# A two-layer graph network in fp32 on one core: new places for the weights, the first three and the last two graphs

## The chip, the core and the metric

The kernel runs on one core of a Trainium2 chip. The metric is the device time of one execution in microseconds (us). The program uses five instruction streams: TensorE (PE in the profile; its weight loads are listed apart as PEld), VectorE (DVE), ScalarE (ACT), GpSimd (POOL), and SyncE (SP), which here only issues DMAs. Each stream runs its instructions strictly in the order in which they were written; an instruction that has to wait holds up all that stand behind it in its stream.

## The reference, cut to what matters

There are 64 graphs of 256 nodes with 512 features each, in fp32. All graphs use the same weights: W0 (512 x 1024), Wv (512 x 512), aw (1024 x 1), Wk (3 x 512 x 512), and three small biases.

```python
# layer 0
h = relu(layernorm(x))                                  # over the 512 features
agg = (adj @ h) / max(sum(adj, -1), 1e-6)
x = x + relu(concat([h, agg], 2) @ W0.T)

# layer 1
h = relu(layernorm(x))
Xw = h @ Wv + bv
e = leaky_relu((Xw @ aw[:512])[:, None, :] + (Xw @ aw[512:])[:, :, None] + ab, 0.2)
alpha = adj * exp(e)
T = alpha / (sum(alpha, -1) + 1e-12)                    # "transition"
H = h @ Wk[0] + bk[0] + (T @ h) @ Wk[1] + bk[1] + (T @ (T @ h)) @ Wk[2] + bk[2]
out = x + relu(H)
```

## The kernel before, in words

**The arithmetic.** All the large products are taken apart in Strassen's manner: a product of two matrices in 2x2 blocks becomes seven block products, with sums of blocks of the left and the right factor before, and sums of the results behind. Weights are combined once at the start and stay in SBUF (`W0F`, `W1F`, `WQF`; the profile calls them all `l` or `lq`). For each graph TensorE makes products of 256 columns with a weight tile of 128x128, each in one step from SBUF to a PSUM bank; VectorE and ScalarE pass the partial sums between banks and SBUF, and GpSimd makes most of the sums of the left factors and some sums of results. The layer-1 product is regrouped: h times v (v is Wv times the two halves of aw, in two rows) gives the two scores of a node without forming Xw, and T·(h·Wk[1] + T·h·Wk[2]) is summed in one set of banks with h·Wk[0].

**The stages of a graph**, with the names that are used below (lines of the kernel before):
- `prepare` (L534): `norm_relu` (L316) on x: row sums with ScalarE, the scaling of the mean `sm` (POOL, L329), squares (ACT, L331), the variance and its power -0.5 (POOL, L333 and L334), then the scaled ReLU (ACT, L337), giving h in tile `h0`. `scaled` (near L520) divides the adjacency by its row sums. Both must then be transposed. For graphs 0 and 1, `flip_on_pe` (L363) does this with TensorE transposes into a bank and copies out of it; for the others, `put` (L340) transposes blocks of 32x32 on VectorE (L345) and writes them to DRAM by DMAs on SP (L349), and `get` (L353) reads them back in the transposed order in the stage `prepared` (L545).
- `wide` (L555): h times both halves of W0, as a scheme of 26 products. `LEFT_SUMS` are 18 sums of 128x128 blocks of h-transposed, one instruction each (L387 on VectorE or L389 on GpSimd); `EARLY` (graphs 0 and 1, banks 3 to 6) and `STEPS` (the others, banks 0 to 2) list the products and the passing of the partial sums: P a product, S a copy to a staging tile, D, T and O sums, F a copy back to a bank.
- `layer0` (L597): the aggregation as seven products through `main` (L494) on banks 0 to 2, started by its "fifth" product; `finish` (L512) adds the ReLU of the banks to x (L516).
- `turn1` (L607): layernorm and ReLU of the new x, four dot products with the v rows on VectorE (L613), and `put` of h to DRAM.
- `transition` (L622): the column of scores goes out and comes back as a row through DRAM (L624, L625); four exponentials (L630), the maximum of the two branches (L633), two products with the adjacency, the scaling, and the transposition: for graphs 1 to 61 through DRAM, for graph 0 and the last two on TensorE (`tt.flip`, L373).
- `moved`, `once`, `inner`, `turned1`, `outer` (from L647): the sums of the transition (tile `st`), `spread` (L446, T times h as seven pairs of 128x128 products on banks 6 and 7, giving `zg`), `inner` (L659, banks 6 and 7, times the third weight, giving `qf`), the read of h-transposed, and `outer` (L687, banks 3 to 5, everything added up), whose `finish` and one DMA of 512 KB per graph (L694) store the output.

In a turn of the loop, `moved` to `outer` run for the graph before, `prepare` and `prepared` for the next graph, and the loads of x and adjacency (L314) for the graph three ahead.

**The order of the work.** Nothing is ordered by the compiler. Each operation is recorded by `Plan.add` (L200) with its engine and the tiles that it reads and writes. `emit` (L222) sorts the operations of each engine by a place, and writes them in that order:

```python
at = self.base + (times[self.count] if self.count < len(times) else 0.0)   # base: graph * TURN + SHIFT
for i in sorted(range(len(self.ops)), key=lambda i: self.ops[i][3]):       # emit
```

The places stand in the table `AT`, a row for each stage; graphs 0 to 2 have rows of their own (`wide_0`), graphs 62 and 63 in two stages, and `SHIFT` moves whole stages of the last four graphs. A place decides only the order in a stream, not a time. The costs given to `add` have no effect on the program.

**The start.** `first` (L823) loads x of graph 0 in halves. `weights_l0` (L708) loads W0 in four parts of 512 KB (L712), transposes it with 8 groups of four transposes into banks 1, 2 and 0 in rotation (L725), and copies each half bank to SBUF by ScalarE (16 copies, L731 and L733). `combine0` (L736) makes 28 sums of these pieces on VectorE. `weights_l1` (L744) loads and transposes Wv (L775), copies it (L777), and multiplies it with aw: aw is broadcast to a 128-wide tile (L768), so that each of the two products of 512 columns gives a v row already repeated in all 128 partitions. Then `combine` (L698, L703) forms sums of Wk, and bk is spread by one product with ones. `pool_op` (L385) decides which of the sums run on VectorE instead of GpSimd: all those of graph 0, and `zg`, `qf` and `st` of graph 1.

Of the kernel before, what the change touches and what calls it, by code (L numbers as in the profile page):

```python
# [11 lines left out]
AF = mybir.ActivationFunctionType  # L12
# [13 lines left out]
TURN = 44.55  # L26
AT = {
    "first": (-1017.24, -941.27, -1067.90, -979.42, -1133.31, -1447.98, -1153.03, -1322.56, -861.36, -1000.46, -1271.51, -1112.17, -1031.96,
        -1007.46, -997.64, -1019.48, -995.91, -966.87, -807.55, -710.53, -781.12, -671.89, -691.05, -715.55, -741.64, -649.04, -668.80, -637.21,
        -513.09, -573.30, -611.16, -532.37, -616.22, -652.18, -1057.15, -794.26, -597.00, -1140.64, -889.40, -650.49, -823.54, -717.73, -1031.47,  # L30
        -761.68, -747.99, -593.69, -583.75, -527.52, -656.78, -632.97, -239.87, -431.83, -275.83, -1179.40, -946.09, -433.84, -905.70, -638.56,
        -569.10, -880.53, -782.04, -705.59, -492.83, -421.05, -288.74),
    "inner": (112.00, 118.30, 113.21, 111.00, 119.38, 119.48, 120.51, 123.95, 119.91, 117.78, 125.62, 122.20, 129.97, 123.35, 122.08, 122.94, 143.35),
    "inner_0": (120.04, 124.14, 111.34, 108.02, 121.17, 121.28, 127.27, 128.59, 125.03, 116.12, 137.98, 117.98, 127.36, 129.02, 121.84, 124.49,
        158.46),
    "inner_1": (116.30, 120.49, 114.79, 118.55, 119.44, 121.25, 125.68, 131.77, 125.03, 121.31, 129.70, 128.89, 139.17, 129.13, 123.63, 129.21,
        153.96),
    "inner_2": (117.14, 119.66, 118.60, 112.70, 119.26, 121.13, 124.83, 125.54, 119.49, 118.09, 129.51, 123.19, 123.50, 122.53, 120.98, 119.85,
        132.84),
    "layer0": (8.82, 12.23, 23.66, 30.27, 32.06, 29.03, 34.55, 32.01, 36.75, 34.14, 40.29, 34.61, 40.44, 41.44, 41.62, 36.17, 36.49),  # L40
    "layer0_0": (-200.51, -154.12, -17.22, -72.28, 8.54, -32.05, 23.63, -26.42, 30.82, -16.30, 32.72, -9.73, 34.62, 34.67, 35.87, -8.32, -3.57),
    "layer0_1": (-17.97, 4.41, -34.79, 12.11, 32.36, 15.72, 43.05, 22.64, 44.10, 24.61, 47.37, 27.04, 47.39, 47.89, 48.17, 27.25, 27.35),
    "layer0_2": (16.51, 27.98, 24.87, 29.85, 39.27, 28.73, 40.14, 29.55, 40.49, 31.62, 41.67, 35.42, 41.84, 41.86, 44.64, 35.47, 36.33),
    "loads": (-73.25, -54.78),
    "loads_2": (-570.55, -440.31),
    "moved": (96.10, 94.60, 90.90, 91.65, 92.10, 98.61),
    "moved_0": (74.40, 78.92, 73.46, 86.50),
    "moved_1": (91.74, 94.49, 96.28, 96.47, 101.59, 99.65),
    "moved_2": (92.45, 93.46, 87.17, 93.36, 88.66, 95.64),
    "moved_late": (277.68, 282.26, 301.99, 292.62),  # L50
    "once": (54.49, 60.96, 71.27, 72.69, 100.45, 102.13, 97.01, 101.40, 103.69, 104.26, 107.89, 108.15, 102.72, 101.65, 111.96, 103.21, 108.87,
        104.14, 109.67, 110.05, 110.23),
    "once_0": (61.39, 68.65, 43.72, 76.81, 102.31, 108.28, 88.12, 81.94, 109.93, 110.01, 111.86, 113.88, 100.99, 87.31, 97.51, 91.16, 118.80, 101.72,
        103.42, 103.65, 107.11),
    "once_1": (66.98, 69.71, 84.14, 73.11, 100.43, 102.58, 97.12, 100.84, 104.63, 106.78, 110.21, 112.55, 110.97, 102.83, 112.58, 108.30, 112.06,
        106.52, 108.00, 110.24, 114.90),
    "once_2": (48.31, 85.20, 76.99, 85.55, 99.90, 100.10, 96.57, 97.65, 102.25, 103.85, 102.31, 107.68, 98.75, 105.26, 111.34, 111.29, 114.34,
        108.24, 109.43, 112.02, 115.28),
    "outer": (110.55, 112.56, 124.59, 130.71, 122.70, 126.64, 130.05, 124.51, 132.31, 132.69, 134.42, 130.55, 136.29, 137.75, 137.79, 134.66, 140.16,
        142.97, 144.27, 143.30, 141.14, 144.88, 147.05, 147.31, 154.75, 166.76, 149.89, 152.90, 180.04, 173.32, 178.81, 183.03),  # L60
    "outer_0": (75.64, 100.62, 136.69, 136.53, 104.98, 130.05, 133.80, 126.65, 135.71, 136.92, 137.86, 135.82, 139.47, 140.60, 141.14, 138.11,
        143.83, 144.28, 144.84, 145.15, 143.50, 148.77, 148.79, 152.22, 164.19, 164.74, 149.82, 155.17, 176.64, 177.49, 176.45, 180.92),
    "outer_1": (116.86, 117.84, 128.53, 124.70, 122.55, 133.39, 134.11, 129.95, 135.65, 136.44, 136.94, 134.18, 139.81, 139.88, 141.12, 136.84,
        143.12, 148.89, 149.66, 146.81, 143.91, 148.56, 149.77, 153.75, 159.49, 159.72, 152.49, 156.26, 164.38, 167.52, 171.63, 187.33),
    "outer_2": (109.82, 117.34, 125.19, 132.21, 122.42, 127.44, 130.36, 123.94, 131.81, 132.14, 134.85, 131.51, 136.29, 138.25, 138.62, 135.11,
        140.08, 141.11, 142.64, 144.31, 139.88, 144.08, 146.43, 149.56, 150.02, 152.80, 151.35, 151.79, 159.27, 158.56, 152.70, 181.89),
    "prepare": (-58.85, -58.04, -62.77, -50.47, -50.61, -50.10, -47.67, -44.00, -35.79, -33.31, -40.71, -40.92, -34.53, -30.46, -9.67, -12.00,
        -30.84, -30.59, -19.83, -17.85, -13.42, -16.63, -13.01, -0.86, -2.11, 0.02, -0.84),
    "prepare_0": (-1266.53, -975.17, -811.01, -687.47, -880.33, -683.51, -631.06, -581.34, -621.45, -471.77, -1128.62, -1029.34, -1034.44, -882.61,
        -476.14, -489.14, -495.72, -471.07, -383.05, -399.08),  # L70
    "prepare_1": (-557.96, -458.29, -573.61, -253.06, -248.24, -448.75, -390.09, -379.42, -209.99, -190.33, -642.97, -325.85, -355.58, -242.70,
        -180.44, -173.98, -131.68, -163.72, -123.16, -162.03),
    "prepare_2": (-239.11, -208.13, -283.36, -178.85, -105.45, -128.88, -95.37, -80.24, -60.94, -70.06, -131.95, -63.34, -57.66, -46.88, -50.72,
        -47.06, -39.69, -38.58, -74.39, -50.57, -47.70, -74.26, -35.20, -31.13, -44.27, -36.41, -25.44),
    "prepared": (-10.65, 2.40, -0.87),
    "prepared_0": (-266.03, -448.40, -238.28, -282.28),
    "prepared_1": (-42.49, -39.69, 9.83, -23.75),
    "prepared_2": (-15.15, -0.37, 11.90),
    "transition": (55.63, 60.89, 66.16, 59.33, 66.37, 62.85, 61.19, 61.54, 61.61, 62.29, 62.78, 69.44, 69.86, 65.50, 84.98, 85.82, 78.93, 86.06),
    "transition_0": (-37.87, -34.45, 59.61, 61.95, 59.61, 59.97, 69.12, 70.02, 69.57, 70.91, 71.09, 73.37, 74.08, 94.36, 73.26, 95.01, 76.83),  # L80
    "transition_1": (41.14, 59.01, 60.68, 59.69, 61.21, 66.18, 58.69, 58.69, 58.88, 60.76, 61.81, 69.31, 69.66, 62.81, 83.27, 81.85, 79.74, 81.08),
    "transition_2": (48.98, 68.97, 59.08, 59.45, 64.06, 66.35, 59.35, 61.89, 61.81, 62.34, 62.37, 69.62, 73.39, 66.89, 81.35, 84.81, 82.67, 86.91),
    "transition_late": (-54.45, -49.51, 1.31, -11.56, 5.58, 1.28, 1.86, 18.81, 4.03, 18.88, 19.04, 24.08, 44.52, 30.73, 24.06, 60.74, 64.88),
    "turn1": (34.41, 40.31, 39.20, 37.21, 37.30, 39.30, 43.54, 44.94, 46.57, 47.03, 54.64, 55.20, 55.64, 56.82, 51.30, 51.88, 64.71, 63.98, 58.81,
        56.74),
    "turn1_0": (-37.13, -10.01, -7.88, -26.00, -25.40, -17.44, 11.38, 11.78, 24.35, 28.13, 30.44, 32.22, 43.73, 49.19, 23.26, 23.32, -152.13, -56.73,
        -93.40, -120.59),
    "turn1_1": (23.38, 31.87, 33.04, 29.38, 31.30, 34.45, 39.81, 41.29, 33.66, 34.98, 42.54, 47.50, 58.19, 58.12, 39.23, 35.62, 58.55, 66.38, 62.43,
        46.18),
    "turn1_2": (38.62, 40.24, 40.52, 41.94, 43.04, 43.41, 41.83, 46.90, 48.66, 49.26, 50.41, 54.34, 53.15, 56.69, 48.74, 51.03, 53.76, 56.22, 66.90,  # L90
        64.83),
    "turned1": (112.10,),
    "turned1_0": (76.53,),
    "turned1_1": (120.50,),
# [33 lines left out]


LEFT_SUMS = (  # L130
    (8, '-', 3, 7), (9, '+', 1, 8), (10, '+', 2, 8), (11, '-', 5, 9), (12, '-', 0, 4), (13, '-', 6, 12),
    (14, '-', 2, 13), (15, '+', 1, 3), (16, '+', 4, 6), (17, '+', 16, 15), (18, '-', 5, 12), (19, '-', 1, 18),
    (20, '+', 4, 5), (21, '+', 7, 16), (22, '+', 2, 3), (23, '+', 22, 20), (24, '+', 0, 22), (25, '-', 6, 10),
)
# [764 lines left out]
```

## Time and profile before

| | before |
|---|---|
| runs | 2546.61, 2547.19, 2549.0 us; median 2547.19 |
| profiled execution, its own time | 2546.46 us |
| span in the profile (first to last instruction) | 2544.7 us, 40786 instructions |
| granted TensorE clock, mean | 0.998 of full speed |
| busy: PE, PEld | 2505.8 us (98%), 2211.5 us (87%), 12414 instructions each |
| busy: DVE, ACT, POOL | 1677.1 us (66%), 1317.8 us (52%), 1688.7 us (66%) |
| DMA | 297.95 MB, 117 GB/s on average |

The table gives for the whole span what each engine was busy. The ends differ from the middle, and the page's picture in 40 slices of 63.6 us each shows it (busy tenths; 9 stands for 90% or more, the second line is the granted clock, the third the share of the DMA engines):

```profile
PE   7899999999999999999999999999999999999998
PEclk9999999999999999999999999999999999999999
DMA  4454454454454454454554554544544544545421
```

PE is under 90% only in the first two slices and in the last. The instruction groups of the page that the prediction draws prices from are these (line, engine, operation, output and inputs, shape, count; busy time in all and mean ns of one; idle time before them and what ended it):

```profile
L588 DVE TENSOR_TENSOR bank<-bank,stg 128x256 f32<-128x256 f32 x514 | 214.4, 428 | 213.5 <-PE bank L426 146.5
L389 POOL TENSOR_TENSOR s<-h0t,s 128x128 f32<-128x128 f32 x620 | 313.2, 514 | 0.0
L389 POOL TENSOR_TENSOR s<-h0t 128x128 f32<-128x128 f32 x372 | 199.3, 551 | 7.2 <-DMA h0t<-dh 7.2
L329 POOL TENSOR_SCALAR sm<-sm 128x2 f32<-128x2 f32 x128 | 29.5, 230 | 197.6 <-DVE x L516 138.9
L516 DVE SCALAR_TENSOR_TENSOR x<-bank,x 128x512 f32<-128x512 f32 x256 | 166.4, 686 | 10.4 <-PE bank L426 9.7
```

A product that starts a chain in a bank has to wait until the last reader of the bank is through; such waits show in the column on the right. The idle time of an engine that is not the bound costs nothing.

### The profile page before, as it was taken

Reading aid. Unit: us, or ns where it says so; the run is one execution under the profiler, and the core shown is the slowest. Engines: PE = TensorE matmul, PEld = TensorE weight load, DVE = VectorE, ACT = ScalarE, POOL = GpSimd, SP = SyncE. Lnnn points to the kernel's source line nnn. Section 1 sums busy time; section 2 is a strip of 40 time slices with the busy share of each in tenths; the row PEclk is TensorE's granted clock in tenths of the full one; section 3 lists DMA queues with packets and bytes.
Section 4 is the critical chain, followed back from the end, with each engine's and each line's share of the span. In section 5 each row is a group of like instructions: output and inputs, shape, how many; then the busy total and the mean of one; then the engine's idle time right before and its main releaser. Section 6 shows DMA issues by size and latency. Waiting matters only on the chain.

```text
span 2544.7 us, 40786 instructions
## 1 busy us (share of the span) xinstructions
PE 2505.8 (98%) x12414; PEld 2211.5 (87%) x12414; DVE 1677.1 (66%) x4179; ACT 1317.8 (52%) x3490; POOL 1688.7 (66%) x3162
## 2 busy tenths in 40 slices
PE   7899999999999999999999999999999999999998
PEld 5688888888888888888888888888888888888886
DVE  5777666666666666666666666666666666666653
ACT  6555555555555555555555555555555555555521
POOL 3557766667667677667667667667666676676653
PEclk9999999999999999999999999999999999999999
DMA  4454454454454454454554554544544544545421
GB/s 137 113 128 121 114 126 118 117 128 113 115 135 113 114 127 118 119 121 115 128 121 112 128 123 112 128 119 118 125 113 119 132 112 115 133 109 121 114 67 44
DMA packets 576912, 297.95 MB, mean 117 GB/s; under 512 B 419251, under 2 KB 542899, under 8 KB 576694
## 3 DMA queue, kind: packets, MB, share of 16 engines
q1 hardware_dynamic: 576694, 295.35, 47.7%
q8 instruction: 99, 1.62, 0.3%
q14 instruction: 119, 0.97, 0.2%
HBM read 163.33 MB, written 131.92 MB: 116 GB/s over the span
## 4 chain that ended last, share of the span: by engine, by line
PE 95%; DMA 1%; DVE 1%; issue 1%; ACT 0%; POOL 0%; SPq 0%; DVEq 0%; POOLq 0%; ACTq 0%
PE bank L426 95%; DMA h0t<-dh 0%; DMA l<-in_L_gnn_Wv_dram 0%; DMA dh<-turned 0%; DMA x<-in_x_dram 0%; ACT stg L438 0%; POOL hf L389 0%; SPq L314 0%; DVE x L516 0%; POOL s L389 0%; DVE turned L345 0%; PE bank L775 0%; DVE z L613 0%; PE bank L373 0%; DVE stg L588 0%
## 5 line engine op out<-in xcount | busy, mean ns | idle before, releaser
L426 PE MATMUL bank<-l,s 128*128 128x256 f32 x3292 | 877.4, 380 | 6.8 <-DVE bank L441 2.9
L426 PEld LDWEIGHTS bank<-l,s 128*128 128x128 f32 x3292 | 609.2, 190 | 93.2 <-POOL s L389 3.9
L438 ACT COPY stg<-bank 128x256 f32<-128x256 f32 x958 | 342.8, 372 | 508.7 <-PE bank L426 188.2
L426 PE MATMUL bank<-l,zg 128*128 128x256 f32 x1820 | 468.1, 380 | 3.6 <-POOL zg L389 1.5
L426 PE MATMUL bank<-lq,zg 128*128 128x256 f32 x1792 | 448.2, 379 | 1.2 <-DVE zg L441 0.9
L426 PEld LDWEIGHTS bank<-lq,zg 128*128 128x128 f32 x1792 | 339.8, 190 | 49.5 <-DVE zg L441 1.5
L426 PEld LDWEIGHTS bank<-l,zg 128*128 128x128 f32 x1820 | 336.2, 190 | 45.7 <-POOL zg L389 1.7
L389 POOL TENSOR_TENSOR zg<-zg 128x256 f32<-128x256 f32 (+1 forms) x187 | 133.7, 728 | 355.2 <-ACT zg L438 343.3
L588 DVE TENSOR_TENSOR bank<-bank,stg 128x256 f32<-128x256 f32 x514 | 214.4, 428 | 213.5 <-PE bank L426 146.5
L389 POOL TENSOR_TENSOR s<-h0t,s 128x128 f32<-128x128 f32 x620 | 313.2, 514 | 0.0
L426 PE MATMUL bank<-l,h0t 128*128 128x256 f32 x1008 | 289.5, 380 | 2.1 <-DVE q L588 1.1
L426 PEld LDWEIGHTS bank<-l,h0t 128*128 128x128 f32 x1008 | 197.3, 196 | 25.1 <-DVE q L588 1.5
L613 DVE SCALAR_TENSOR_TENSOR z<-h1n,v_sb 128x512 f32<-128x512 f32 x256 | 200.0, 781 | 11.0 <-ACT h1n L337 2.7
L389 POOL TENSOR_TENSOR s<-h0t 128x128 f32<-128x128 f32 x372 | 199.3, 551 | 7.2 <-DMA h0t<-dh 7.2
L426 PE MATMUL bank<-l,h1t 128*128 128x256 f32 x784 | 202.1, 379 | 1.8 <-DVE lo L444 1.8
L438 ACT COPY qf<-bank 128x256 f32<-128x256 f32 x128 | 47.6, 372 | 291.1 <-DVE qf L441 258.7
L331 ACT ACTIVATE h1n<-x,sm 128x512 f32<-128x512 f32 x130 | 92.9, 715 | 158.9 <-POOL sm L329 158.9
L516 DVE SCALAR_TENSOR_TENSOR x<-bank,x 128x512 f32<-128x512 f32 x256 | 166.4, 686 | 10.4 <-PE bank L426 9.7
L426 PEld LDWEIGHTS bank<-l,h1t 128*128 128x128 f32 x784 | 152.8, 196 | 19.4 <-DVE lo L444 2.6
L329 POOL TENSOR_SCALAR sm<-sm 128x2 f32<-128x2 f32 x128 | 29.5, 230 | 197.6 <-DVE x L516 138.9
L426 PE MATMUL bank<-q,sa 128*128 128x256 f32 x512 | 153.6, 382 | 2.7 <-DVE bank L441 2.0
L389 POOL TENSOR_TENSOR qf<-qf 128x256 f32<-128x256 f32 x124 | 90.9, 733 | 98.2 <-DVE qf L441 98.2
(170 smaller groups left out, 4584.5 us busy)
## 6 DMA issues: line engine op xcount, KB each, us to landing
dh<-turned SPq DMA_DIRECT2D x504, 128.0 KB, 3.3
h1t<-dh SPq DMA_DIRECT2D x64, 512.0 KB, 3.9
out_dram<-x SPq DMA_DIRECT2D x64, 512.0 KB, 3.1
x<-in_x_dram SPq DMA_DIRECT2D x63, 512.0 KB, 4.6
h0t<-dh SPq DMA_DIRECT2D x62, 512.0 KB, 4.2
a<-in_adj_dram SPq DMA_DIRECT2D x64, 256.0 KB, 4.4
dan<-turneda SPq DMA_DIRECT2D x248, 64.0 KB, 1.9
raw<-dan SPq DMA_DIRECT2D x62, 256.0 KB, 2.7
```

The costliest lines, as they stand in the source:

```text
L329: add("POOL", 0.23, lambda: nc.gpsimd.tensor_scalar(sm, sm, -1.0 / F, None, op0=ALU.mult), [], parts(smk))
L331: add("ACT", 0.9, lambda c=c: nc.scalar.activation(h[:, c, :], s[:, c, :], AF.Square, bias=sm[:, c : c + 1], accum_out=sq[:, c : c + 1]), ...
L389: add("POOL", cost, lambda: getattr(nc.gpsimd, f)(to, p, q), reads, [write])
L426: nc.tensor.matmul(ps, lhs, rhs, start=start, stop=True, skip_group_check=True)
L438: add("ACT", 0.37, lambda: nc.scalar.copy(dst, bank[b][:, cols]), [f"bank{b}"], dkeys)
L516: add("DVE", 0.75 if sums else 0.69, lambda c=c: nc.vector.scalar_tensor_tensor(t[:, c, :], bank[banks[1 + c]], 0.0, t[:, c, :], op0=ALU.m ...
L588: add("DVE", 0.43, lambda f=f, to=to, x=x, y=y: getattr(nc.vector, f)(to, x, y), pbk + [k], tok)
L613: add("DVE", 0.83, lambda s=s, c=c: nc.vector.scalar_tensor_tensor(scr.rearrange("p c n -> p (c n)"), h[:, c, :], 1.0, v_sb[:, s, :], op0= ...
```

## The change

1. **The table.** `AT`, `TURN` and `SHIFT` are all new. The last two graphs have rows of their own in every stage (`_late`, `_last`); all shifts are zero.
2. **W0.** It is transposed into eight banks, one group of four transposes each, instead of three in rotation. Seven of its sixteen pieces (`IN_PSUM`) are not copied to SBUF: the sums that need them read the bank. Nine ScalarE copies are left. x of graph 1 is issued on SP ahead of W0, W0's third and fourth parts come before its first two, and both adjacency matrices follow W0.
3. **Sums of h.** The 18 sums become nine instructions of twice the size (128x256, two blocks at once, with a stride between the blocks given by `pair`); a few of the 18 are other sums than before, and `LEFT` is renumbered for them. Graph 0's sums of h, of the adjacency, of h in layer 1 (`hf`) and `s1` go to GpSimd; `zg`, `qf`, `st` and the last sums of `wide` stay on VectorE. In graphs 62 and 63 `zg`, `qf`, `st` and `hf` go from GpSimd to VectorE.
4. **The mean's scaling** (`sm`, two per graph) goes from GpSimd to ScalarE.
5. **The v rows.** aw is used as it comes, two columns wide: one product of 512 columns gives both rows, each in one partition; two short products with a selecting matrix (`sel`) repeat them in all partitions, and the constant is made in the same way. The sums of the third weight (`lq`, four) go from VectorE to GpSimd.
6. **Graphs 1 and 2.** `wide` of graph 1 has its own staging tiles, `layer0` of graph 1 uses banks 3 to 5, and h of graph 2 is transposed on TensorE (banks 0 and 1) instead of through DRAM.
7. **The last output.** Graph 63's `outer` uses banks 6 and 7 as well. Its four quarters of 128x256 are finished by one sum each and stored by a DMA of 128 KB each, in place of two sums of 128x512 and one DMA.

The diff, without the rows of `AT`:

```diff
-TURN = 44.55
+TURN = 38.52
...
+IN_PSUM = (27, 29, 31, 33, 35, 36, 37)
...
 LEFT_SUMS = (
-    (8, '-', 3, 7), (9, '+', 1, 8), (10, '+', 2, 8), (11, '-', 5, 9), (12, '-', 0, 4), (13, '-', 6, 12),
...
+    ((8, 9), '-', (0, 3), (4, 7)), ((10, 11), '+', (1, 2), (9, 9)), ((12, 13), '-', (5, 6), (8, 8)),
+    ((14, 15), '-', (5, 6), (10, 11)), ((16, 17), '-', (1, 2), (12, 13)), ((19, 20), '+', (1, 2), (3, 3)),
+    ((18, 21), '+', (4, 4), (5, 6)), ((22, 23), '+', (18, 19), (20, 21)), ((24, 25), '+', (0, 7), (20, 21)),
...
 # norm_relu
-        add("POOL", 0.23, lambda: nc.gpsimd.tensor_scalar(sm, sm, -1.0 / F, None, op0=ALU.mult), [], parts(smk))
+        add("ACT", 0.22, lambda: nc.scalar.mul(sm, sm, -1.0 / F), [], parts(smk))
...
     def pool_op(f, cost, to, p, q, reads, write):
-        if plan.graph < 2 and write[:2] in ("zg", "qf", "st") and plan.name[:4] != "wide" or plan.graph == 0:
+        if plan.graph < 2 and writes[0][:2] in ("zg", "qf", "st") and plan.name[:4] != "wide" or plan.graph == 0 and writes[0][:2] == "q0" or (
+                plan.graph >= G - 2 and writes[0][:2] in ("zg", "qf", "st", "hf")):
...
     def main(terms, banks, seeds, keys, fifth, last=None):
+        if last:
+            x, y = banks[3:]
+            plus(bank[x][:, lo], [f"bank{x}"], p, lo, s21[:, 1], keys[1:])
+            last(1, hi, x, lo)
+            plus(bank[d][:, lo], [f"bank{d}"], p, lo, s21[:, 0], keys[:1])
+            step(2, r, lo, terms)
+            add("ACT", 0.37, lambda: nc.scalar.copy(bank[y][:, lo], bank[r][:, hi]), [f"bank{r}"], [f"bank{y}"])
+            last(0, lo, r, lo)
+            step(3, y, lo, terms)
+            last(0, hi, y, lo)
+            step(4, d, lo, terms)
+            last(1, lo, d, lo)
+            return
...
 # prepare, prepared
+        if g < 3:
+            flip_on_pe(h, F, tr_banks if g < 2 else itertools.cycle((0, 1)), H0T[0] if g != 1 else H1T[0])
+        else:
+            put(h, F, TURNED[0], of(D["h0"], g))
...
 # wide
+        def pair(a, b):
+
+            (x, xk), (y, yk) = left[a], left[b]
+            if a == b:
+                return x.unsqueeze(1).to_broadcast([P, 2, P]), xk
+            step = y.offset - x.offset
+            return bass.AP(tensor=x.tensor, offset=x.offset, ap=[list(x.ap[0]), [step, 2], list(x.ap[-1])]), xk + yk
...
+        if g == 1:
+            stage = [(MZ[0][0][:, i], f"{MZ[0][1]}.{i}") for i in range(3)] + [(lo5[:, 1], "lo5.1")]
...
 # layer0
-        (p0, pk), banks = P0[0], (0, 1, 2)
+        (p0, pk), banks = P0[0], (0, 1, 2) if g != 1 else (3, 4, 5)
...
 # outer
+        def last(c, cols, b, at):
+            part = t[:, c, cols], f"{k}.{c}{cols.start}"
+            add("DVE", 0.43, lambda: nc.vector.scalar_tensor_tensor(part[0], bank[b][:, at], 0.0, part[0], op0=ALU.max, op1=ALU.add),
+                [f"bank{b}", f"{k}.{c}"], [part[1]])
+            add("SP", 0.4, lambda: nc.sync.dma_start(out[g, c * P : (c + 1) * P, cols], part[0]), [part[1]], [f"out{g}.{part[1]}"], 2.2)
...
 # weights_l0
-        for n in (0, 2, 1, 3):
-            for kk in range(0, FC, 2):
-                b = next(banks)
+        for n, kk, b in ((0, 0, 0), (0, 2, 1), (2, 0, 6), (2, 2, 5), (1, 0, 2), (1, 2, 4), (3, 2, 3), (3, 0, 7)):
...
+                if f in IN_PSUM:
+                    assert sign > 0
+                    ps[f] = bank[b][:, cols], f"bank{b}"
+                elif sign > 0:
+                    copy(form[f][0], [form[f][1]], b, cols)
...
 # weights_l1
-        add("ACT", 1.1, lambda: nc.scalar.copy(awb, awc.unsqueeze(3).to_broadcast([P, 2, FC, P])), ["awc"], awbk)
+        add("ACT", 0.4, lambda: nc.scalar.copy(sel, ident[:2, :2].unsqueeze(2).to_broadcast([2, 2, P])), ["ident"], ["sel"])
...
+        def product(b=b):
+            for oc in range(FC):
+                matmul(bank[b][:2, :], awc[:, :, oc], wvt[oc][0], oc == 0)
+        add("PE", 3.45, product, ["awc"] + [f"wvt{oc}" for oc in range(FC)] + wvt[0][1] + wvt[2][1], [f"bank{b}"])
+        add("ACT", 0.6, lambda b=b: nc.scalar.copy(vrow[:, :F], bank[b][:2, :]), [f"bank{b}"], vrk)
...
         for s in range(2):
             b = next(banks)
-                    matmul(bank[b], awb[:, s, oc, :], wvt[oc][0], oc == 0)
+            add("PE", 0.9, lambda b=b, s=s: matmul(bank[b], sel[:, s], vrow[:, :F], True), vrk + ["sel"] + zk, [f"bank{b}"])
...
-            add("DVE", 0.97, lambda to=to, f=f, p=p, q=q: getattr(nc.vector, f)(WQF[to], p, q), pk + qk, [f"lq_{to}"], port=True)
+            add("POOL", 1.3, lambda to=to, f=f, p=p, q=q: getattr(nc.gpsimd, f)(WQF[to], p, q), pk + qk, [f"lq_{to}"], port=True)
```

For the order in the streams, the two tables give this. For a graph that is neither among the first three nor the last two, TensorE, VectorE and SP run the same operations in the same order as before; GpSimd runs 39 operations a graph instead of 50, ScalarE two more. At the start SP issued W0 (parts 1 and 0), the adjacency of graph 0, the first half of its x, W0 (3), the second half of x, W0 (2), x of graph 1, a part of Wk, and aw. Now it issues x of graph 1, W0 (3), the first half of graph 0's x, W0 (2), the second half, W0 (1 and 0), bv, the adjacencies of graphs 1 and 0, then the parts of Wk and Wv and the small vectors; aw is 27th.

## The prediction

> **What bounds the kernel now.** I read the page first, then the busy time by stretches, then TensorE's timeline at both ends.
>
> ```profile
> span 2544.7 us, 40786 instructions
> PE 2505.8 (98%) x12414; PEld 2211.5 (87%) x12414; DVE 1677.1 (66%) x4179; ACT 1317.8 (52%) x3490; POOL 1688.7 (66%) x3162
> ...
> PE 95%; DMA 1%; DVE 1%; issue 1%; ACT 0%; POOL 0%; SPq 0%; DVEq 0%; POOLq 0%; ACTq 0%
> ```
>
> TensorE is the bound and the others have slack. The stretches say where it is not:
>
> ```profile
> 10.00:20.00 10.00, 4.73 (x21) 3.31 (x20) 5.52 (x18) 9.65 (x29) 1.39 (x4) 0.92 1.10 340
> 20.00:30.00 10.00, 8.29 (x36) 6.53 (x37) 5.58 (x21) 5.08 (x14) 1.91 (x2) 0.74 0.73 232
> 70.00:80.00 10.00, 7.27 (x23) 5.21 (x24) 8.03 (x22) 4.13 (x11) 4.76 (x6) 0.83 0.79 202
> 400.00:800.00 400.00, 400.00 (x2000) 356.26 (x1999) 266.79 (x666) 211.93 (x562) 275.79 (x515) 1.00 0.51 121
> ```
>
> From 130 to 2400 us the list of TensorE's waits is empty; only both ends can give. Two outputs, issued at 2317.03 and 2355.55, give 38.52 us a graph. That is 89 products of 256 columns at 0.432 (four records in 0.865). I add TensorE's work in queue order at this pace (0.43 for four transposes, 3.46 for four products of 512 columns): 2485.7 us in all. Where it stands, less the work queued before, is the time lost so far:
>
> ```profile
> 21.49 2.82 PE L775 MATMUL bank<-ident,l 128*128 128x128 f32 x12 [5.11 <-DMA l<-in_L_gnn_Wv_dram]
> 24.96 1.16 PE L426 MATMUL bank<-l,h0t 128*128 128x256 f32 x4
> ...
> 79.96 0.38 PE L373 MATMUL bank<-ident,an 128*128 128x128 f32 x2
> ...
> 115.86 1.14 PE L426 MATMUL bank<-l,h0t 128*128 128x256 f32 x4 [0.36 <-DVE x L516]
> ...
> 2485.11 6.64 PE L426 MATMUL bank<-lq,zg 128*128 128x256 f32 x28 [0.26 <-DVE zg L441]
> ...
> 2515.35 7.00 PE L426 MATMUL bank<-lq,zg 128*128 128x256 f32 x28 [0.62 <-DVE zg L441]
> ```
>
> Lost: 19.3 at the first wide product (24.96, 5.6 of work), 33.5 where graph 0's transition is flipped (79.96, 46.4), 43.4 at graph 3 (115.86, 72.4), 45.3 at graph 62's inner (2485.11), 50.8 at graph 63's (2515.35), 59.0 at the end. The reader is to see 43 us lost before graph 3, 1 in sixty graphs, 14.6 behind them.
>
> **The change part by part.**
>
> *The middle.* I sorted both tables of places. For a graph that is not among the first three or last two, TensorE, VectorE and SP keep their order exactly; only sums are merged, and the mean's scaling goes to ScalarE. On GpSimd 18 sums of h, 9.2 us a graph (569.5 us over 62), become 9, at 0.73 to 0.85 (its 128x256 rows) 6.6 to 7.7. ScalarE gets 2 x 0.22. I take 0: TensorE's continuous work hides both, and GpSimd had a third of its time idle. Without that cover it costs what TensorE waits, times 60.
>
> *TensorE's work.* The v rows need one product of 3.46 and two broadcasts of 0.86 (the row of bk) instead of two of 3.46; the constant 1.2 instead of 1.9; two flips of graph 2 add 0.86. Sum -1.6.
>
> *To the first wide product.* Now SP issues x of graph 1 (0.5 MB) before W0, with halves 2, 3 before 0, 1. In the trace 1 MB had landed at 5.7 us and 6.25 MB at 21.5: 0.345 MB/us. So W0.2 and 3 stand at 7.9 (1.75 MB), W0.0 and 1 at 11.5 (3 MB). Eight groups of four transposes at the cold 0.93 (12 in 2.79) run 7.9 to 10.7 and 11.5 to 16.1; before, the last ended at 14.85, so 1.3 later. But nine copies instead of sixteen leave the banks (7 x 0.36 of ScalarE), and graph 0's flips follow W0 at once, where before three transposes of Wv stood between and waited for their DMA. ScalarE, queued behind the adjacency of graph 1 (12.2), finishes the first ReLU at 17.6 and the copy at 18.9. The product then waits until sum 15 has read bank 4. VectorE's sums wait for copy 30 at 17.9 and run 0.35 apart: 19.9. Lost 15.6, before 19.3.
>
> *Wide and layer 0 of graph 0.* Eighteen small sums (0.29) leave VectorE for GpSimd in pairs; four lq sums (0.68) too, at 1.2 (half of L703's 2.36). The chain product, copy, sum on four banks is the limit, as it was. The one product for v waits for wvT copy four (29.6) and for aw, now 27th on SP and issued near 24; awc took 7.8 us to land at the start, so 28 to 31. Everything in TensorE's queue stands behind it; I take 1 us. Following the banks, layer 0's fifth product starts at 43.3 (before 48.79), x is finished at 52 (before 57.2).
>
> *Graphs 1 and 2.* Own staging for graph 1 and banks 3 to 5 for its layer 0 let wide 1 and wide 2 interleave; graph 2's h no longer goes out and back:
>
> ```profile
> 81.14 0.76 POOL L389 TENSOR_TENSOR s<-h0t 128x128 f32<-128x128 f32 x2 [6.38 <-DMA h0t<-dh]
> ```
>
> From x finished to the scaled transition graph 0 took 57.2 to 78.4, 21.2 us (squares, ReLU, two dot products, two DMAs of 3.5 and 3.9, four exponentials, sums). From 52 that gives 73 to 74, where TensorE has 48.7 of work behind it: lost 25.3, before 33.5. What is late next: the copy of the flip's second half on ScalarE and sum st0 on VectorE stand behind graph 1's ReLU and dot products. Those end 8 us after its layer 0 (73.8), so the spread starts at 80 to 82 and TensorE waits 4.4. Before, it stalled between 81 and 112 in eight pieces. Lost 30 at the inner of graph 0; with 3 more for the following small waits, 33 at graph 3.
>
> *GpSimd beside VectorE.* What this walk lacks is seen here: a VectorE sum from SBUF, 0.42 elsewhere, beside a large GpSimd sum.
>
> ```profile
> 46.30 2.16 DVE L387 TENSOR_TENSOR q<-q 128x256 f32<-128x256 f32 x1
> ...
> 45.81 2.36 POOL L703 TENSOR_TENSOR l<-l,l 128x1024 f32<-128x1024 f32 x1
> ```
>
> One hit costs up to 1.7. Thirteen GpSimd instructions are new beside the W0 sums and wide 0; many VectorE operands now lie in PSUM, or wait anyway. Between 0 and 9 (13 x 0.7) I take 2, nearest to one such hit; 1 more for a cold clock after the waits. So 36 at graph 3, before 43.4: -7.4. The Trainium skill ("SBUF — State Buffer", section "Who interferes with whom") speaks against the move: a GpSimd read and a VectorE instruction with two SBUF inputs exclude each other for the whole instruction. By that rule alone all thirteen could block, an estimate of 9 lost and a start better by nothing.
>
> *The end.* zg, qf, st and hf of the last two graphs move to VectorE: 0.42 instead of 0.73 there. Graph 63's flips move into graph 62's outer, 20 us of work behind its layer 0; its chain is 19.7 by the rows of 2485 to 2508, so it just fits. The 5.5 lost between the two inners become 2.6 (1.2 in outer 62, the rest around the spread), the 3.4 of the last inner and outer 2.7. The output:
>
> ```profile
> 2511.34 29.85 SPq L694 DMA_DIRECT2D out_dram<-x  x2
> ```
>
> The second is issued at 2540.8 after two sums of 0.69, and the span ends at 2544.7: 4.8 from the last product. A quarter needs one sum of 0.43 and a DMA of 128 KB: between 1.9 (64 KB) and 3.1 (512 KB), I take 2.3. Three quarters are queued ahead on SP, 0.4 each, all issued before. 3.7. Sum of the end -4.7; bounds -8 (no wait left) and +3 (the flips come late by a chain as slow as before's, 22.4).
>
> **Sum.** -1.6 - 7.4 - 4.7 = -13.7. The profiled execution took 2546.46 (span 2544.7), so 2532.8; the median of the runs is 0.73 above it: 2533.5.
>
> **Rivals.**
> *The start gives nothing* (0.18): the first graphs are a chain through ScalarE and VectorE, and VectorE was busy 9.3 of 10 us at 60 to 70. aw landing 4 us later, or the hits on GpSimd taking 7, leaves only TensorE's work and the end: 2547.2 - 6.3 = 2541. For it: W0 really lands later. Against it: the first flip no longer waits for Wv.
> *More* (0.12): VectorE meets no blocks (-3), the spread's 4.4 us fills with wide 2, the end loses nothing more (-4): 2522.
> *Slower* (0.10): a pair sum holds GpSimd 0.73 instead of 0.5, and VectorE's dot products and maxima beside it grow in every graph; TensorE then waits once a graph. From 0.23 us a graph (13.7 over 60) this eats everything; at 0.4 it is 2557. Against it: no wait in 2270 us, an unchanged order, GpSimd 2 us freer. A middle that does not follow the tables would show here too.
>
> **How the numbers follow.** My case (0.60) lies between 2526 and 2541. The range from 2521 to 2546 leaves out half of "more" (0.06) and the slower case (0.10) and holds the other 0.84. 0.2% is 5.1 us, about what a measurement can tell from no change: faster is below 2542.1. Mine, "more" and half of the first rival make 0.80; its other half 0.10 same; slower 0.10.
>
> **What would show it.** First wide product at 20 (+-1.5) and no wait on Wv; graph 0's flip at 74; a wait of about 4 us at the spread, behind ScalarE or VectorE; no wait on aw above 2; graph 3's first product near 110; none from 130 to 2400; 3.7 from the last product to the end. Wrong if TensorE waits in the middle, or graph 3 starts after 116.

## The result, and the profile after

The changed kernel takes 2558.78 us (median of 5 runs, 2557.57 to 2560.34), the kernel before beside it 2546.61 us. The ratio is 1.0045, 95% interval 1.0034 to 1.0056: 12 us slower, where 13.7 us faster was forecast. The profiled execution took 2558.45 us, its span is 2556.7 us.

The page of the changed kernel, its first lines and the chain's shares by engine:

```profile
span 2556.7 us, 40160 instructions
PE 2516.4 (98%) x12412; PEld 2209.8 (86%) x12412; DVE 1697.3 (66%) x4172; ACT 1336.4 (52%) x3616; POOL 1557.0 (61%) x2466
...
PE 96%; DVE 1%; DMA 1%; issue 1%; ACT 0%; SPq 0%; POOL 0%; DVEq 0%
```

On this level nothing is wrong: TensorE is the bound as before, and GpSimd has lost 132 us of work. The busy time by stretches shows more (stretch in us, its length, and the busy time of TensorE, weight loads, VectorE, ScalarE and GpSimd):

```profile
10.00:20.00 10.00, 5.12 (x32) 4.00 (x30) 5.28 (x15) 7.88 (x25) 2.19 (x5) 0.97 0.99 331
20.00:30.00 10.00, 9.06 (x40) 7.46 (x41) 7.70 (x21) 7.43 (x24) 6.71 (x14) 0.69 0.78 240
70.00:80.00 10.00, 6.85 (x22) 4.49 (x20) 8.13 (x20) 4.00 (x12) 6.08 (x10) 0.83 0.00 0
400.00:800.00 400.00, 398.75 (x1975) 353.09 (x1974) 267.98 (x661) 213.26 (x578) 252.09 (x400) 1.00 0.49 121
```

From 10 to 30 us the start is better filled, from 70 to 80 us it is not (6.85 us of TensorE's work, 7.27 before). And in the middle TensorE is now busy 398.75 of 400 us, where before it was 400.00. The stores of the output, one a graph, are issued at 2213.91 and 2252.80: 38.89 us a graph in place of 38.52. Most of the lost time is thus hidden in the share of busy time: 1.25 us in 400 show as idle, while 10.3 graphs x 0.37 are 3.8 us; the rest lies in products that count as busy for longer behind the wait. The list of TensorE's waits from 130 to 2400 us, empty before, now has one line (us in total, times, longest):

```profile
PE bank L464 <- DVE bank L479: 0.9, 2, 0.5
```

It shows 0.9 us where some 21 are lost: an almost empty list of waits does not say that nothing was lost.

TensorE's timeline at the places that the prediction used (start, length, engine, line, operation; in brackets the idle time before, and what ended it):

```profile
20.94 1.22 PE L464 MATMUL bank<-l,h0t 128*128 128x256 f32 x2 [1.47 <-DVE l L821]
...
31.17 3.59 PE L464 MATMUL bank<-l,awc 128*2 128x512 f32 x8
...
78.57 0.38 PE L409 MATMUL bank<-ident,an 128*128 128x128 f32 x2
...
112.72 0.59 PE L464 MATMUL bank<-l,h0t 128*128 128x256 f32 x2
...
2497.82 1.03 PE L464 MATMUL bank<-lq,zg 128*128 128x256 f32 x4
...
2529.13 1.13 PE L464 MATMUL bank<-lq,zg 128*128 128x256 f32 x4 [0.52 <-DVE zg L479]
```

These are the first wide product, the product of aw for the v rows, the flip of graph 0's transition, the first product of graph 3, and the first product of `inner` for graphs 62 and 63. The place of each, less the work that stands before it in TensorE's queue (4.32, 48.72, 74.73, 2435.63 and 2462.94 us, 2484.1 in all, added up as in the prediction), is the time lost so far. The last column is the third experiment below (the first-product and flip times there are 20.89 and 78.27):

| TensorE's lost time, us | before | predicted | changed kernel | e3 |
|---|---|---|---|---|
| first wide product | 19.3 | 15.6 | 16.6 | 16.6 |
| flip of graph 0's transition | 33.5 | 25.3 | 29.9 | 29.6 |
| graph 3's first product | 43.4 | 36 | 38.0 | 37.7 |
| inner of graph 62 | 45.3 | 37.9 | 62.2 | 40.6 |
| inner of graph 63 | 50.8 | 40.5 | 66.2 | 44.6 |
| end of the span | 59.0 | 46.9 | 72.6 | 51.3 |

(The predicted values below graph 3 follow from its terms: 1.9 in the middle as before, then 2.6, 2.7 and 3.7 with the rest of the tail.) The start gained what was forecast within 2 us, the tail most of it. Between graph 3 and graph 62, where the prediction took 0, 24.2 us are lost in place of 1.9.

Where in a graph? Once in each turn TensorE stops ahead of the last products of `layer0`. First the same place in the kernel before, all engines in time order, with only the lines of this step:

```profile
1229.15 0.43 DVE L441 TENSOR_TENSOR bank<-bank,p 128x256 f32<-128x256 f32 x1 [1.05 <-PE bank L426]
...
1229.82 0.59 PE L426 MATMUL bank<-q,sa 128*128 128x256 f32 x2
...
1230.09 0.42 DVE L441 TENSOR_TENSOR qf<-bank,qf 128x256 f32<-128x256 f32 x1 [0.18 <-PE bank L426]
1230.25 1.03 PE L426 MATMUL bank<-l,zg 128*128 128x256 f32 x4
1230.45 0.43 DVE L441 TENSOR_TENSOR bank<-bank,p 128x256 f32<-128x256 f32 x1
1230.55 0.37 ACT L438 COPY qf<-bank 128x256 f32<-128x256 f32 x1 [4.35 <-DVE qf L441]
...
1231.11 0.59 PE L426 MATMUL bank<-q,sa 128*128 128x256 f32 x2
...
1231.54 0.59 PE L426 MATMUL bank<-q,ant 128*128 128x256 f32 x2
```

And the changed kernel:

```profile
1232.11 0.60 PE L464 MATMUL bank<-q,sa 128*128 128x256 f32 x2
1232.31 0.37 ACT L476 COPY qf<-bank 128x256 f32<-128x256 f32 x1 [3.73 <-PE bank L464]
...
1232.54 1.03 PE L464 MATMUL bank<-l,zg 128*128 128x256 f32 x4
...
1232.78 0.42 DVE L479 TENSOR_TENSOR qf<-bank,qf 128x256 f32<-128x256 f32 x1 [0.58 <-ACT qf L476]
1233.12 0.42 DVE L479 TENSOR_TENSOR bank<-bank,p 128x256 f32<-128x256 f32 x1
...
1233.66 0.30 PEld L464 LDWEIGHTS bank<-q,sa 128*128 128x128 f32 x2 [0.50 <-issue]
1233.69 0.67 PE L464 MATMUL bank<-q,sa 128*128 128x256 f32 x2
...
1234.20 0.60 PE L464 MATMUL bank<-q,ant 128*128 128x256 f32 x2
```

In `inner`, ScalarE copies a part of the result (t3 in the code) out of the low half of a bank, and VectorE adds the same half to another part (b11) to form a third (t2); all lie in the tile qf. Neither reads what the other writes, and in both kernels they still run one behind the other. Before, VectorE's sum came first (1230.09, as soon as TensorE was done) and the copy waited for it: ScalarE had time. Now the copy comes first, and the sum waits for it until 1232.78. Behind the sum in VectorE's queue stands the sum of `layer0` (bank<-bank,p), and TensorE's next product waits for that: 0.29 us of stop (the products before it, from 1232.54, were done at 1233.40 at the pace of before, 0.86 for these four records), and 0.51 instead of 0.43 until the next group of products starts. Together 0.37 us, the difference between 38.89 and 38.52.

Why the order turned over can be read from `emit`. It goes round the engines in turn, and on each writes all that is ready (an operation is ready when all that it depends on has been written). The turn is the order in which the engines first come up in the sorted places. In the table before, ScalarE had the earliest place, then SP, TensorE, VectorE, GpSimd; in the new one VectorE, TensorE, GpSimd, SP, ScalarE. When TensorE's products for the bank have been written, the next engine in the round that reads the bank is VectorE in the first case and ScalarE in the second. Followed through `emit`, the sum is written first in all 64 graphs before, the copy in 59 of 64 now. The order on TensorE, VectorE and SP is the same in both, but for exchanges of neighbours in a few graphs.

The Trainium skill bears on it ("PSUM — Partial Sum Buffer", section "PSUM bank collisions raise a hardware error"): two engines may not be on the same bank and partitions at once, two readers included, and the compiler's scheduler puts a dependency between any two such instructions. The rows above agree as far as they go: the two never overlap, and the second starts 0.04 (before) and 0.10 us (now) behind the end of the first. No run here shows what would happen without the wait.

### The profile page after: what moved, and what is told of

It reads as the page before. It is cut to its first block, busy times and chain, and to the rows that moved or that the text cites. A ratio compares the mean times of both kernels' runs of the same rounds, so it can differ in the third digit from the quotient of the medians.

```text
span 2556.7 us, 40160 instructions
## 1 busy us (share of the span) xinstructions
PE 2516.4 (98%) x12412; PEld 2209.8 (86%) x12412; DVE 1697.3 (66%) x4172; ACT 1336.4 (52%) x3616; POOL 1557.0 (61%) x2466
## 4 chain that ended last, share of the span: by engine, by line
PE 96%; DVE 1%; DMA 1%; issue 1%; ACT 0%; SPq 0%; POOL 0%; DVEq 0%
PE bank L464 96%; DMA a<-in_adj_dram 0%; DMA dtt<-turneda 0%; DMA dh<-turned 0%; DVE bank L657 0%; DVE bank L479 0%; SPq L385 0%; PE bank L409 0%; DVE st L425 0%; DVE l L821 0%; PE bank L855 0%; DVE q L657 0%; ACT mz L476 0%; SPq L791 0%; DVE qf L479 0%
## 5 line engine op out<-in xcount | busy, mean ns | idle before, releaser
L427 POOL TENSOR_TENSOR zg<-zg 128x256 f32<-128x256 f32 x180 | 128.8, 729 | 358.9 <-ACT zg L476 335.4
L427 POOL TENSOR_TENSOR s<-h0t,s 128x256 f32<-128x256 f32 x315 | 233.6, 742 | 0.4
L682 DVE SCALAR_TENSOR_TENSOR z<-h1n,v_sb 128x512 f32<-128x512 f32 x256 | 208.1, 813 | 12.3 <-ACT h1n L373 3.8
L427 POOL TENSOR_TENSOR qf<-qf 128x256 f32<-128x256 f32 x120 | 111.7, 931 | 141.9 <-DVE qf L479 141.9
L464 PE MATMUL bank<-qf,st 128*128 128x256 f32 x512 | 152.5, 380 | 0.3 <-DVE qf L425 0.2
L427 POOL TENSOR_TENSOR s<-h0t 128x256 f32<-128x256 f32 x189 | 143.6, 774 | 12.0 <-ACT h0t L415 8.0
L427 POOL TENSOR_TENSOR q<-q 128x256 f32<-128x256 f32 x189 | 136.0, 734 | 16.6 <-DVE q L657 16.6
```

Of the source, the lines that this page charges most:

```text
L427: add("POOL", cost, lambda: getattr(nc.gpsimd, f)(to, p, q), reads, writes)
L464: nc.tensor.matmul(ps, lhs, rhs, start=start, stop=True, skip_group_check=True)
L682: add("DVE", 0.79, lambda s=s, c=c: nc.vector.scalar_tensor_tensor(scr.rearrange("p c n -> p (c n)"), h[:, c, :], 1.0, v_sb[:, s, :], op0= ...
```

## The experiments

The theory is then: the order of these two readers costs 0.365 us a graph. The rivals are the pieces of work that did move in every graph: the sums of h in pairs on GpSimd, which the prediction had named as the way to a slower kernel, and the mean's scaling on ScalarE.

**e1, the changed kernel with the turn of the kernel before.**

```diff
 # Plan.emit
-        queues = {}
+        queues = {e: [] for e in ("ACT", "SP", "PE", "DVE", "POOL")}
```

> The changed kernel, but emit goes round the engines in the order ScalarE, SP, TensorE, VectorE, GpSimd, as the program before did, instead of VectorE, TensorE, GpSimd, SP, ScalarE. Every engine's own order stays. Theory (the order in which emit writes the copy of t3 and the sum t2, which read the same bank, decides which of the two waits): 38.52 us a graph, and 58 graphs x 0.365 us come back: 2558.8 - 21.2 = 2537.6, between 2535 and 2540. Rival (work moved between ScalarE and GpSimd lengthens every graph): 38.89 a graph and 2558.8.

Measured: 2539.69 us, ratio to the kernel before 0.9968 (0.9956 to 0.9979), 38.52 us a graph. TensorE's work, the tables and each engine's order are those of the changed kernel, so the moved work costs TensorE nothing in the middle. The span is 2538.3; graph 3 starts at 113.82, 1.1 us later than in the changed kernel, after W0 was first used at 9.34 instead of 7.92. Why it was later is not explained.

**e2, the kernel before with the turn of the changed kernel.**

```diff
 # Plan.emit of the kernel before
-        queues = {}
+        queues = {e: [] for e in ("DVE", "PE", "POOL", "SP", "ACT")}
```

> The kernel before, but emit goes round the engines in the order VectorE, TensorE, GpSimd, SP, ScalarE. Nothing else. Theory (order of the two readers): 38.89 us a graph, 2546.6 + 58 x 0.365 = 2567.8, between 2564 and 2571. Rival (moved work): 38.52 a graph and 2546.6.

Measured: 2571.83 us, ratio 1.0093 (1.0079 to 1.0107), 38.89 us a graph. This is 23.5 us above the runs of the kernel before that stood beside it (2548.36); the middle gives 59 x 0.365 = 21.5, and graph 3 starts at 118.40 instead of 115.86, so the turn costs 2.5 us in the first graphs too; with these the whole lies 0.8 us above the range that was expected. The stretch of the middle and the pair:

```profile
400.00:800.00 400.00, 398.74 (x1987) 353.46 (x1986) 264.48 (x660) 210.07 (x556) 274.49 (x515) 1.00 0.49 120
```

```profile
1242.07 0.37 ACT L438 COPY qf<-bank 128x256 f32<-128x256 f32 x1 [3.82 <-PE bank L426]
1242.54 0.42 DVE L441 TENSOR_TENSOR qf<-bank,qf 128x256 f32<-128x256 f32 x1 [0.58 <-ACT qf L438]
```

With nothing of the change in it, the kernel before loses the same time at the same place.

**e3, only this pair held in order.**

```diff
 # inner
         copy(*t3, bx, lo)
         plus(*t2, bx, lo, *b11)
+        if OWN <= g < G - 2:
+            plan.ops[-2][2].add(len(plan.ops) - 1)      # the copy is written after the sum
```

> The changed kernel with its own engine order; only the copy of t3 is held until the sum t2 has been written, for graphs 3 to 61. Theory (this pair alone costs the 0.365 us): 38.52 a graph, 2558.8 - 21.2 = 2537.6; if other pairs share in it, between 2537.6 and 2558.8. Rival (moved work): 2558.8.

Measured: 2537.06 us, ratio 0.9958 (0.9945 to 0.9970), 38.52 us a graph: 0.42% faster than the kernel before. One pair of readers is the whole 0.365 us a graph.

```profile
400.00:800.00 400.00, 400.00 (x1990) 356.36 (x1989) 270.43 (x665) 213.25 (x578) 255.95 (x406) 1.00 0.49 120
```

```profile
1261.09 0.42 DVE L479 TENSOR_TENSOR qf<-bank,qf 128x256 f32<-128x256 f32 x1 [0.18 <-PE bank L464]
1261.45 0.43 DVE L479 TENSOR_TENSOR bank<-bank,p 128x256 f32<-128x256 f32 x1
1261.55 0.37 ACT L476 COPY qf<-bank 128x256 f32<-128x256 f32 x1 [4.26 <-DVE qf L479]
```

The sum goes ahead again, and ScalarE waits.

**e4, GpSimd's work as before.**

```diff
 # wide: each pair sum as two instructions
-            pool_op("tensor_add" if op == "+" else "tensor_sub", 0.8, to, x, y, xk + yk, keys)
+            f = "tensor_add" if op == "+" else "tensor_sub"
+            def run(f=f, to=to, x=x, y=y):
+                for j in range(2):
+                    getattr(nc.gpsimd, f)(to[:, j], x[:, j], y[:, j])
+            add("POOL", 0.8, run, xk + yk, keys)
 # norm_relu
-        add("ACT", 0.22, lambda: nc.scalar.mul(sm, sm, -1.0 / F), [], parts(smk))
+        on_pool = OWN <= g < G - 2
+        add("POOL" if on_pool else "ACT", 0.22, lambda: nc.gpsimd.tensor_scalar(sm, sm, -1.0 / F, None, op0=ALU.mult)
+            if on_pool else nc.scalar.mul(sm, sm, -1.0 / F), [], parts(smk))
```

> The changed kernel, with each pair sum of h as two instructions of 128x128 again (all graphs) and the mean's scaling on GpSimd again (graphs 3 to 61). Theory (order of the two readers): nothing comes back, 38.89 a graph, 2558.8 within 1.5. Rival (pair sums, or the scaling on ScalarE, lengthen every graph): 38.52 a graph and about 2537.6.

Measured: 2564.55 us, ratio 1.0065 (1.0051 to 1.0078), 38.89 us a graph. Nothing comes back, so the rival falls. It is even slower than the theory's 2558.8 +- 1.5 allowed, and not in the middle: graph 3 starts at 117.30, 4.6 us later than in the changed kernel, behind one wait of TensorE that the changed kernel doesn't have:

```profile
67.09 0.70 PE L465 MATMUL bank<-l,s 128*128 128x256 f32 x2 [3.92 <-POOL s L637]
```

In the first graphs the sums of h in pairs are worth some 4 us: without them GpSimd is late for a wide product. The start's gain over the kernel before, 5.4 us of lost time, would nearly be gone (43.4 before, 42.6 here).

**e5, another tile for t3.** Is it the bank that the two share, or the tile qf into which both write?

```diff
 # inner
         b11, b21, b22, t4, nt1, t2, t3 = (at(i) for i in range(7))
+        t3 = t3own, ["t3own"]                           # a tile of its own, 128 x 256
```

> The changed kernel, but the copy of t3 goes to a tile of its own instead of a seventh part of qf. It still reads the same bank as the sum t2. If the two wait for each other because of the bank: nothing changes, 38.89 us a graph and 2558.8 within 1.5. If because both write parts of the tile qf: 38.52 a graph and about 2537.

Measured: 2558.46 us, ratio 1.0042 (1.0028 to 1.0056), 38.89 us a graph. The two still follow each other, so it is not the tile; what they still share is the bank (both read the same half of it, and no run has them read different halves):

```profile
1231.14 0.37 ACT L477 COPY t3own<-bank 128x256 f32<-128x256 f32 x1 [3.73 <-PE bank L465]
1231.61 0.43 DVE L480 TENSOR_TENSOR qf<-bank,qf 128x256 f32<-128x256 f32 x1 [0.58 <-ACT t3own L477]
```

**e7, the rest written by place.**

```diff
 # Plan.emit, with the pair held as in e3
+            ready = [(self.ops[q[heads[e]]][3], e) for e, q in queues.items() if heads[e] < len(q) and self.ops[q[heads[e]]][2] <= done]
-            for e, queue in queues.items():
-                while heads[e] < len(queue) and self.ops[queue[heads[e]]][2] <= done:
-                    i = queue[heads[e]]
+            for _, e in sorted(ready)[:1]:
+                i = queues[e][heads[e]]
...
```

> The changed kernel with the pair t2, t3 held in order for graphs 3 to 61; in all else emit writes, of the instructions that are ready, the one with the earliest place, in place of going round the engines. Theory (in the middle the pair alone matters, so only the start and the last graphs can move): 38.52 a graph, 2537.1 within 3. Rival (other pairs of readers in the middle matter too): more than 38.52 a graph.

Measured: 2540.15 us, ratio 0.9966 (0.9954 to 0.9977), 38.52 us a graph, at the upper edge of what was expected. The middle loses nothing in this order of writing either. The start is no better (graph 3 at 112.78), so this order finds nothing more there.

**e9, the adjacency behind the first ReLU.** With the pair held as in e3:

```diff
 # first: places of the loads of a of graph 0, x of graph 1, a of graph 1
-40.65, -62.78, 17.53, -93.73, 10.95),
+40.65, -62.78, 10.95, -93.73, 17.53),
 # prepare_1: place of the first row sum of the adjacency
-5.28, 10.75, -55.80, -20.79,
+5.28, 10.75, -20.84, -20.79,
```

> The changed kernel with the pair held in order; on ScalarE one row sum of graph 1's adjacency stands behind the first ReLU of graph 0 instead of before it, and SP issues graph 0's adjacency ahead of graph 1's. The prediction let the first ReLU wait for that adjacency. If it does (1.2 us of idle ScalarE at 11.8 to 13.0): the first flip of h starts at 16.3 instead of 17.5 to 18, the first wide product 1 us earlier, the whole 2536 to 2537. If the copies of W0 and VectorE's sums set that product: 2537.1 within 1.

Measured: 2538.26 us beside 2549.84 for the kernel before, ratio 0.9957 (0.9945 to 0.9970). The first product came when the first hypothesis said (the flip at 16.45), one us earlier than in e3:

```profile
16.45 0.66 PE L409 MATMUL bank<-ident,h0n 128*128 128x128 f32 x4 [1.65 <-ACT h0n L373]
...
19.94 0.71 PE L464 MATMUL bank<-l,h0t 128*128 128x256 f32 x2 [1.47 <-DVE l L823]
```

Its profile carries the gain through (graph 3 at 110.72, span 2533.7 against 2535.4 in e3), but the median lies above the 2536 to 2537 that was expected, and the ratio can't be told from e3's. Both beat the two kernels.

## Why the prediction was wrong

*The middle: wrong, and alone decisive.* The step that failed is: "For a graph that is not among the first three or last two, TensorE, VectorE and SP keep their order exactly ... I take 0". The statement holds, but for exchanges of neighbours (two products of TensorE in each of six turns of the first third, some operations in graphs 57 to 61); the conclusion does not. What was compared was the order on each engine; what was not looked at is the order between engines in which `emit` writes, and that decides which of two readers of a bank waits for the other. The row that hid it is "the list of TensorE's waits is empty" from 130 to 2400 us: it says that nothing was late, not how little was missing. Counted from the start of the products of `layer0` (1229.82 before, 1232.11 now), the sum of `layer0` on VectorE started 0.63 us behind them before and 1.01 now, and TensorE's next product 1.29 and 1.58: a delay of 0.38 us stopped TensorE for 0.29, so only 0.1 us had been to spare. Of the 59 graphs one is graph 63, which the middle does not hold. Measured: 58 graphs x 0.365 = 21.2 us in place of 0; with the 2.9 that e3 loses between graph 3 and graph 62 this makes 24.1 of the 24.2 in the table.

*The slower rival: near in its price by luck, wrong in its mechanism.* "From 0.23 us a graph this eats everything; at 0.4 it is 2557." It came to 0.365 us and 2558.8, of which some 4 us do not come from this pair (the start, the tail and 1.0 us in between gave less than forecast). But GpSimd was not the cause: e4 takes the pair sums apart and still loses 0.365 us, e1 and e3 keep them and lose nothing. VectorE's dot products beside GpSimd's larger instructions did get longer, 813 ns instead of 781, and so did GpSimd's own sums of qf, 931 instead of 733; but in e3, where the middle loses nothing, they take 825 and 934. That rival's last sentence (a middle that does not follow the tables) was nearer, with 0.10 for the whole.

*The start: right within 2 us, by errors that cancel in part.* The first wide product at 20.94 (forecast 19.9), still behind a sum on VectorE, and no wait on Wv, as forecast. Graph 0's flip at 78.57, not 74: the chain from x to the transition was taken as 21.2 us and ran 24.7 (from the last sum of x, done at 53.91). Part of it lies in three instructions of VectorE beside GpSimd's sums:

```profile
72.14 1.15 DVE L702 TENSOR_TENSOR z<-z,z 128x512 f32<-128x512 f32 x1
...
73.89 0.95 DVE L704 SCALAR_TENSOR_TENSOR z<-z,a 128x256 f32<-128x256 f32 x1
...
74.88 0.73 DVE L706 TENSOR_SCALAR tot<-tot 128x2 f32<-128x2 f32 x1
```

The same three before:

```profile
75.33 0.69 DVE L633 TENSOR_TENSOR z<-z,z 128x512 f32<-128x512 f32 x1
...
76.63 0.42 DVE L635 SCALAR_TENSOR_TENSOR z<-z,a 128x256 f32<-128x256 f32 x1
...
77.09 0.17 DVE L637 TENSOR_SCALAR tot<-tot 128x2 f32<-128x2 f32 x1
```

They are 1.55 us longer now, beside GpSimd's power and sums (72.02 to 75.6). That looks like the hindrance that the prediction booked with 2 us, three times in one chain, and about of that size in sum; no run takes GpSimd's work away there to show it. The rule that was weighed there (the Trainium skill, "SBUF — State Buffer", "Who interferes with whom") fits the first two rows in kind, with two inputs in SBUF each; the third has one, and is not covered by it. By the estimate of 9 us that went with it the start would have gained nothing, and it gained 5.4. The stall at the spread, forecast 4.4, came as waits of 0.46, 0.46, 0.17 and 1.75 us, 2.8 in all; the first is behind ScalarE's copy of the transition and the last behind VectorE's sum st, as named. Ahead of it stand two waits that the forecast did not have, 1.25 and 1.31 us (at 80.20 and 83.07), for VectorE's sums q of graph 2's `wide`. The errors cancel in part: 4.6 us more than forecast were lost up to the flip, 8.1 in place of 10.7 from there to graph 3. So graph 3 lost 38.0, forecast 36, and that it is so near is partly luck.

*aw: no wait.* The 1 us taken for the product of the v rows was not needed; it starts at 31.17 with no idle time before it. aw stands 28th on SP, not 27th, and is issued at 22.86.

*TensorE's work, the end.* 1.6 us less work is used in all the sums above; the constant, taken as 1.2 us, took 0.34 and 0.38 in two products. Between the two inners 4.0 us were lost (forecast 2.6, before 5.5), from the last inner to the end of the last product 3.2 (2.7, before 3.4), and from there to the end 3.2 (3.7, before 4.8). In sum the tail gained 3.3, forecast 4.7.

*Without the middle.* In e3 the other terms are, by the table, -1.6 of work, -5.7 to graph 3, +1.0 from there to graph 62 and -3.0 behind it: -9.3, as the spans have it (2544.7 and 2535.4), where -13.7 was forecast. e3's median, 2537.06, lies between 2526 and 2541, where the prediction saw its own case.

## What to carry to other kernels

Where a program is written by a loop over engine queues, the order between engines is part of the schedule: here ScalarE and VectorE, reading one PSUM bank, ran one behind the other in the order in which they were written, and a new table of places can turn that over with every queue unchanged. Compare the whole written order, at least for each pair of instructions that share a bank, and hold the pairs that matter by an explicit dependency. An empty list of waits says nothing of the slack behind it, and a nearly empty one can stand for 21 us (0.9 listed here); look at how long before its use each operand of the bound engine is ready.

## What the runs showed of the hardware

Sums of h in pairs on GpSimd took 742 and 774 ns for 128x256, near the lower end of what the prediction took. Against 514 and 551 ns for each 128x128 before, a pair saves 0.29 and 0.33 us; against the same sums taken apart in e4 (469 and 484 ns each) it saves 0.2. A wait of TensorE costs more than its idle time: behind 0.29 us of stop the next group of products started 0.51 instead of 0.43 us later, and 398.75 busy of 400 us stood for 3.8 us lost.
